# Two graph layers over sixteen graphs: in the first graph, turning through DRAM instead of by TensorE

## The chip, the core and the metric

One core of a Trainium2 chip runs the whole program. The metric is device time in microseconds (us) of one launch. Before the change it is 1216.43 us, the median of three runs (1216.17 to 1216.68).

## What is computed

Sixteen graphs of 1024 nodes with 256 features go through two layers, each with a residual and a layer norm. `adj` is symmetric and holds 0 and 1.

```
# layer 0, per graph
e0    = leaky_relu((h * a0) @ h.T, 0.2)               # 1024 x 1024, symmetric
alpha = sigmoid(where(adj == 1, e0, -max))            # kinds 2 to 4 do not occur
x     = layernorm(x + alpha @ h + bias)
# layer 1, per graph
Hh = x @ W;  s = Hh @ a_src;  d = Hh @ a_dst
e  = where(adj != 0, exp(-leaky_relu(s[:, None] + d[None, :], 0.2)), 0)
x  = layernorm(x + elu(e @ Hh / rowsum(e)))
```

## The kernel before, in words

All matrices are float32. A graph is cut into eight blocks of 128 nodes. `xs` holds the nodes as rows, `xTs` the features as rows (two chunks c of 128), `xas` is `xTs` times `a0`. Because the score matrix is symmetric, only its upper part is computed: `strip(b, jt)` makes block row jt from its diagonal to the right, in chunks of up to 512 columns. For each chunk TensorE makes `pe` (L254), ScalarE takes two tanh of it, `tb` (L262) and `low` (L263), and VectorE keeps the larger (L264). `finish` adds 1 and masks with `adj` into `al` (L270); GpSimd adds twice the identity on the diagonal block (`add_twice`, L284). The lower part of `al` is the strip turned over:

- In graphs 1 to 15 through DRAM. `dump` turns 32 by 32 blocks on VectorE (L290) and sends the strip off in four transfers whose runs are 32 elements long (L294); `gather` reads it back turned, in one transfer (L298); `mask` then adds 1 and masks in place (L305). `dump`, `gather` and most other transfers are issued by SyncE, whose queue is called SP here; they stand in it in the program's order, and an issue that waits holds up those behind it.
- In graph 0 by TensorE. `mirror` turns each 128 by 128 block with the identity into PSUM (L313), and VectorE masks from there (L315).

Graph 0 is done in the plain way. `multiply0(0, t)` sums row block t over eight blocks jt (L396), in the order jt = 0 to 7; for jt over t it reads what was turned. `end0` adds the bias (L405) and takes statistics. Strips run three ahead of the sums. The rows after layer 0's norm are `x1`. Layer 1 needs them turned: the upper half goes to DRAM (`save_x1`, L546), comes back in eight transfers with runs of 32 elements (`fetch_x1`, by `load_blocks`, L122), and VectorE turns the 32 by 32 blocks (`turn_x1`, L557). The lower half is turned by TensorE (`transpose_x1`, L564) and copied by ScalarE (L565). `scale0` normalizes `x1` in place on ScalarE, after `save_x1` has read it. Graph 1's `x` comes turned from DRAM by the same `load_blocks`, is finished on VectorE by `turn_x` (L213) and scaled on ScalarE (L219).

`W` gets two more columns (`make_Wx`: products with both halves of `a`, L188 and L189) and is then centred (`center_Wx`: two matrix products with a matrix of 1/256 into PSUM, L195, and two subtractions, L197).

From graph 1 on, layer 0 of graph b and layer 1 of graph b-1 run interleaved: strips with `project` (L582, layer 1's `x1 @ W`), then Strassen-like block products of `al` and `x` (L477) whose operands VectorE combines (L455), then layer 1's sums over `e` (L642), whose weights VectorE makes (L637). In graph 1, `project` starts at strip 2, behind `transpose_x1`.

The adjacency of a graph is 4 MB of int32, cast to bf16 by transfers that GpSimd issues (L107), on a queue of their own. Before the change those of graphs 0 and 1 are all issued at the start. The engines are scheduled by hand: instructions stand on each engine in the order of the program text.

Of the kernel before, what the change touches and what calls it, by code (L numbers as in the profile page):

```python
# [9 lines left out]
F32 = mybir.dt.float32  # L10
# [4 lines left out]
ALU = mybir.AluOpType  # L15
# [15 lines left out]
def one_kind_pass(  # L31
# [135 lines left out]
    for h in range(2):  # L167
        for g in range(2):
            load_adj(0, g, ts(h, HALF))
    for g in range(2):  # L170
        load_adj(1, g)

    acol = const.tile([P, ND], F32, tag="acol", name="acol")
    bcol = const.tile([P, ND], F32, tag="bcol", name="bcol")
# [13 lines left out]
            nc.vector.tensor_tensor(wprod, Wx[:, c, 2:], a_bc[:, ts(s, D)], ALU.mult)  # L188
            nc.vector.tensor_reduce(Wx[:, c, s : s + 1], wprod, AX.X, ALU.add)  # L189

    def center_Wx():

        pw = ps_t.tile([P, HT, P], F32, tag="t", name="pw").rearrange("p t q -> p (t q)")[:, 0 : D + 2]
        for c in range(ND):
            nc.tensor.matmul(pw, lhsT=mean_w, rhs=Wx[:, c, :], start=(c == 0), stop=(c == ND - 1))  # L195
        for c in range(ND):
            nc.vector.tensor_tensor(Wx[:, c, :], Wx[:, c, :], pw, ALU.subtract)  # L197

# [41 lines left out]
    def strip(b, jt):  # L240


        if jt == 0:
            als[b] = one.tile([P, NT, N], F32, tag="al", name=f"al_{b}")
        width = N - jt * P
        tb = four.tile([P, N], F32, tag="tb", name=f"tb_{b}_{jt}")
        tbs[b, jt] = tb
        n_chunks = -(-width // HALF)
        per = -(-(width // P) // n_chunks) * P
        for n, o in enumerate(range(0, width, per)):  # L250
            w = min(per, width - o)
            pe = ps_e.tile([P, HALF], F32, tag="e", name=f"pe_{b}_{jt}_{n}")
            for c in range(ND):
                nc.tensor.matmul(  # L254
                    pe[:, 0:w],
                    lhsT=xTs[b][:, c, ts(jt, P)],
                    rhs=xas[b][:, c, ds(jt * P + o, w)],
                    start=(c == 0),
                    stop=(c == ND - 1),
                )  # L260
            low = two.tile([P, HALF], F32, tag="low", name=f"low_{b}_{jt}_{n}")
            nc.scalar.activation(tb[:, ds(o, w)], pe[:, 0:w], AF.Tanh, scale=0.5)  # L262
            nc.scalar.activation(low[:, 0:w], pe[:, 0:w], AF.Tanh, scale=0.5 * SLOPE)  # L263
            nc.vector.tensor_tensor(tb[:, ds(o, w)], tb[:, ds(o, w)], low[:, 0:w], ALU.max)  # L264

    def finish(b, jt, c0=0, c1=N, ends=True):


        c0 = max(c0, jt * P)
        nc.vector.scalar_tensor_tensor(  # L270
            als[b][:, jt, c0:c1],
            tbs[b, jt][:, c0 - jt * P : c1 - jt * P],
            1.0,
            adjs[b, jt // HT][:, jt % HT, c0:c1],
            ALU.add,
            ALU.mult,
        )
        if ends and c0 == jt * P:
            add_twice(b, jt)
# [6 lines left out]
    def dump(b, t):  # L286


        tb = tbs[b, t][:, P : N - t * P]
        nc.vector.transpose(tb, tb)  # L290
        mirs[b, t] = dram.tile([N - (t + 1) * P, P], F32, tag=f"mir_{t}", name=f"mir_{b}_{t}")
        v = mirs[b, t].rearrange("(jb j) (a i) -> a j jb i", j=SQ, i=SQ)
        for a in range(P // SQ):
            nc.sync.dma_start(v[a], tb[ts(a, SQ), :].rearrange("p (jb i) -> p jb i", i=SQ))  # L294

    def gather(b, t):

# [131 lines left out]
    def scale0(b, t):  # L429
        scale(x1s[b][:, t, :], *r0s[b][t])  # L430
# [124 lines left out]
    def turn_x1(b, g):  # L555
        v = x1Ts[b][:, :, ts(g, HALF)]
        nc.vector.transpose(v, v)  # L557

    def transpose_x1(b):

        for c in range(ND):
            pt = ps_t.tile([P, HT, P], F32, tag="t", name=f"px1T_{b}_{c}")
            for t in range(HT):
                nc.tensor.transpose(pt[:, t, :], x1s[b][:, HT + t, ts(c, P)], ident)  # L564
            nc.scalar.copy(x1Ts[b][:, c, ts(1, HALF)], pt.rearrange("p t q -> p (t q)"))  # L565

    def project(b, t):

        if t == 0:
# [150 lines left out]

    for g in range(NT // 2):
        transpose_x(0, g)
    bias_bc = const.tile([P, D], F32, tag="bias", name="bias_bc")
# [6 lines left out]
    a_bc = y_kept[:, 0:2, :].rearrange("p t d -> p (t d)")  # L732
    nc.sync.dma_start(a_bc, a[0].partition_broadcast(P))
    Wx = const.tile([P, ND, D + 2], F32, tag="Wx", name="Wx")
    nc.sync.dma_start(Wx[:, :, 2:], W.rearrange("(c p) o -> p c o", p=P))
    strip(0, 0)
    strip(0, 1)
    for jt in range(2):
        finish(0, jt, 0, HALF)
        mirror(0, jt)  # L740
        if jt == 0:
            strip(0, 2)
    for t in range(NT):
        multiply0(0, t)
        for jt in ([0, 1], [2], [3])[t] if t < 3 else []:
            finish(0, jt, HALF, N)
        if t + 3 < NT:
            strip(0, t + 3)
        if t < 2:
            finish(0, t + 2, 0, HALF)  # L750
        elif t + 2 < NT:
            finish(0, t + 2)
        if t + 2 < NT - 1:
            mirror(0, t + 2)
        end0(0, t)
        if t < 2:
            make_Wx(t)
        if t == 4:
            center_Wx()
        if t == 1:  # L760
            new_xT(1)
            load_blocks(xTs[1], x[1], 0, N)
        if 1 <= t <= CHECKS:
            check_adj(0, t - 1)
        if t in (4, 5):
            turn_x(1, t - 4)
        if t == 3:
            save_x1(0, 0)
            fetch_x1(0, 0)
        if t in (5, 6):  # L770
            scale0(0, 2 * t - 10)
            scale0(0, 2 * t - 9)
    load_x(1, [nc.sync])

    for b in range(1, B):
        prev, done = b - 1, b - 2
        last = b == B - 1

        projects = [[], [0, 1], [2, 3], [4, 5], [6, 7], [], [], []]
        if prev == 0:  # L780

            projects = [[], [], [0, 1], [2, 3], [4, 5, 6, 7], [], [], []]
        for jt in range(NT):
            if jt == 4:
                mask(b, 0, 0, HT)
                combine_al(b, 1, 0, 2)
            if jt == 5:
                new_yT(b)
                product(b, 1)
                mask(b, 1, 0, HT)  # L790
                save_p(prev, 0, NT, nc.scalar)
                share_p(prev, 0, NT)
                combine_al(b, 1, 2, 3)
                mask(b, 0, HT)
                mask(b, 1, HT)
                mask(b, 2, 0, HT)
                combine_al(b, 1, 3, HT)
                mask(b, 2, HT)
                if done >= 0:
                    r1s[done] = center(mv1s[done], f"1_{done}", unit=1.0 / D)  # L800
            if jt == 6:
                unite(b, "p1")
                product(b, 5)
                unite(b, "p5")
                combine_al(b, 2, 0, HT)
            ahead = jt == 0 and b > 1
            if not ahead:
                strip(b, jt)
            if jt == 5:
                mask(b, 3, HT)  # L810
            if not ahead:
                finish(b, jt, ends=False)
            if jt == 4:
                gather(b, 3)
            if jt < NT - 1 and not ahead:
                dump(b, jt)
            if jt < 2 and done >= 0:
                deviation1(done, NT - 2 + jt)
            if prev == 0 and jt == 0:
                turn_x1(0, 0)  # L820
            if prev == 0 and jt == 1:
                transpose_x1(0)
            if ahead:
                gather(b, 0)
            if jt >= (1 if b == 1 else 2) and jt != 4:
                gather(b, jt - 1)
            if jt < 4 and b == 1:
                combine_x(b, jt)
# [653 lines left out]
```

## Time and profile before

| | |
|---|---|
| median of three runs | 1216.43 us |
| profiled execution, its own time | 1216.93 us |
| its span, first to last instruction | 1215.1 us |
| granted TensorE clock | 0.998 |
| TensorE busy | 1205.0 us |
| VectorE busy | 1003.9 us |
| ScalarE busy | 834.3 us |
| first instruction of graph 1's strips on TensorE | 53.7 us |
| last product of graph 1 (L477), first sum of layer 1 (L642) | 98.7 us, 102.1 us |

The span is cut into waits and work for each engine. An engine that is not on the chain of work that ended last may wait without cost, until what it is late with is needed. Two things change with the stage: in graph 0 TensorE is fed from x and the strips alone, with VectorE half busy; from about 60 us on VectorE is busy almost without a break while TensorE also is. Times are counted from the first instruction, so 1.8 us of the profiled execution lie outside the span.

### The profile page before, as it was taken

What the parts mean: (1) busy time and instruction counts of PE and PEld (TensorE: products, weight loads), DVE (VectorE), ACT (ScalarE), POOL (GpSimd) and SP (SyncE); (2) the same over time, 40 slices, a digit from 0 to 9 for tenths busy, and PEclk for the clock granted to TensorE, in tenths of its full rate; (3) what the DMA queues carried; (4) which work ended last, traced back from release to release, by engine and by line L of the source; (5) the groups of instructions that cost most, each with busy time, mean ns of one, the idle gap of its engine ahead of it and who ended that gap; (6) DMA issues with size and microseconds to landing.
All of it is one profiled execution on the core that took longest, in us unless ns stands there. A gap on an engine that the chain in (4) does not pass through costs nothing.

```text
span 1215.1 us, 15998 instructions
## 1 busy us (share of the span) xinstructions
PE 1205.0 (99%) x4385; PEld 819.4 (67%) x4385; DVE 1003.9 (83%) x1774; ACT 834.3 (69%) x2135; POOL 387.1 (32%) x715
## 2 busy tenths in 40 slices
PE   9999999999999999999999999999999999999997
PEld 7757657576575766757667586765757657576686
DVE  5698796988969789697897978979788896988957
ACT  4574866767677666775768757786676767767674
POOL 2320432504334142431414324143250433404343
PEclk9999999999999999999999999999999999999999
DMA  9568778697877878788787886878859788697412
GB/s 195 105 137 151 134 154 169 139 189 132 149 170 139 179 145 157 152 148 179 142 170 137 156 180 130 174 141 150 181 128 189 130 156 170 135 190 133 111 52 73
DMA packets 605080, 180.66 MB, mean 149 GB/s; under 512 B 482612, under 2 KB 587448, under 8 KB 604984
## 3 DMA queue, kind: packets, MB, share of 16 engines
q1 hardware_dynamic: 582800, 136.90, 56.4%
q0 software_dynamic: 20528, 41.95, 18.5%
q8 instruction: 37, 0.61, 0.2%
q10 hardware_dynamic: 1656, 0.72, 0.2%
q14 instruction: 59, 0.48, 0.1%
HBM read 152.44 MB, written 60.62 MB: 175 GB/s over the span
## 4 chain that ended last, share of the span: by engine, by line
PE 90%; DVE 3%; DMA 2%; ACT 2%; issue 1%; SPq 1%; POOL 0%; ACTq 0%; DVEq 0%; POOLq 0%
PE acc L642 33%; PE pe L254 18%; PE pH L582 8%; PE pV L477 8%; PE pQ L477 8%; PE pW L477 8%; PE pR L477 4%; PE acc L396 2%; DMA adj<-in_adjT 1%; DMA al<-mir 1%; DVE al L455 1%; DVE e L637 1%; ACT dev_junk L344 0%; DMA x<-y_rows 0%; DVE al L270 0%
## 5 line engine op out<-in xcount | busy, mean ns | idle before, releaser
L642 PE MATMUL acc<-H,e 128*128 128x257 f32 x2032 | 446.9, 380 | 0.0
L642 PEld LDWEIGHTS acc<-H,e 128*128 128x128 f32 x2032 | 385.1, 190 | 68.8 <-issue 13.9
L254 PE MATMUL pe<-xa,xT 128*128 128x384 f32 (+1 forms) x720 | 249.5, 486 | 0.1
L254 PEld LDWEIGHTS pe<-xa,xT 128*128 128x128 f32 x720 | 133.9, 190 | 91.8 <-issue 52.1
L264 DVE TENSOR_TENSOR tb<-tb,low 128x512 f32<-128x512 f32 (+1 forms) x192 | 112.6, 594 | 62.0 <-ACT low L263 60.1
L637 DVE SCALAR_TENSOR_TENSOR e<-p,pq_kept,adj 128x1024 f32<-128x1024 f32 (+1 forms) x136 | 159.9, 1229 | 0.1
L284 POOL TENSOR_TENSOR al<-ident,al 128x128 f32<-128x128 f32 x128 | 108.9, 864 | 143.1 <-DVE al L270 143.0
L455 DVE TENSOR_TENSOR al<-al 128x1024 f32<-128x1024 f32 (+2 forms) x105 | 143.7, 1369 | 5.1
L262 ACT ACTIVATE tb<-pe 128x512 f32<-128x512 f32 (+1 forms) x192 | 94.1, 490 | 76.6 <-PE pe L254 42.7
L130 ACT ACTIVATE junk<-adj,minus 128x2048 bf16<-128x2048 bf16 x64 | 127.4, 1991 | 0.0
L582 PE MATMUL pH<-Wx,yT 128*128 128x258 f32 x480 | 114.7, 381 | 0.6 <-ACT H L603 0.4
L104 POOL CAST adj<-x 128x1 bf16<-128x1 f32 x15 | 3.2, 213 | 351.6 <-DMA x<-y_rows 274.4
L582 PEld LDWEIGHTS pH<-Wx,yT 128*128 128x128 f32 x480 | 90.9, 190 | 26.7 <-issue 6.0
L477 PE MATMUL pV<-al,S 128*128 128x512 f32 x240 | 107.9, 592 | 0.0
L477 PE MATMUL pW<-al,x 128*128 128x512 f32 x240 | 107.9, 592 | 0.0
L477 PE MATMUL pQ<-al,x 128*128 128x512 f32 x240 | 107.9, 592 | 0.0
L270 DVE SCALAR_TENSOR_TENSOR al<-tb,adj 128x512 f32<-128x512 f32 (+7 forms) x132 | 97.4, 739 | 6.0 <-POOL mr L373 1.0
L668 ACT ACTIVATE sums<-acc,tiny 128x1 f32<-128x1 f32 x45 | 11.8, 262 | 128.0 <-PE acc L642 128.0
L687 ACT ACTIVATE h<-acc,rinv 128x256 f32<-128x256 f32 x81 | 38.2, 471 | 89.1 <-DVE rinv L679 78.1
L263 ACT ACTIVATE low<-pe 128x512 f32<-128x512 f32 (+1 forms) x192 | 95.0, 495 | 1.2 <-DVE tb L264 1.2
L305 DVE SCALAR_TENSOR_TENSOR al<-al,adj 128x512 f32<-128x512 f32 (+3 forms) x150 | 82.5, 566 | 11.7 <-DMA al<-mir 11.7
L477 PEld LDWEIGHTS pW<-al,x 128*128 128x128 f32 x240 | 45.6, 190 | 57.4 <-issue 55.2
(147 smaller groups left out, 1660.9 us busy)
## 6 DMA issues: line engine op xcount, KB each, us to landing
adj<-in_adjT POOLq DMA_DIRECT2D x30, 1024.0 KB, 8.3
x<-in_x SPq DMA_DIRECT2D x15, 1024.0 KB
y_rows<-Z SPq DMA_DIRECT2D x240, 64.0 KB
x<-y_rows SPq DMA_DIRECT2D x30, 512.0 KB
out<-y_kept SPq DMA_DIRECT2D x30, 512.0 KB
xT<-in_x SPq DMA_DIRECT2D x112, 128.0 KB
p<-p_row POOLq DMA_DIRECT2D x15, 512.0 KB, 4.1
mir<-tb SPq DMA_DIRECT2D x60, 112.0 KB
```

Source lines behind the costliest of these rows:

```text
L130: nc.scalar.activation(junk, rows, AF.Square, bias=minus1, scale=2.0, accum_out=chk[:, b * CHECKS + n : b * CHECKS + n + 1],)
L254: nc.tensor.matmul(pe[:, 0:w], lhsT=xTs[b][:, c, ts(jt, P)], rhs=xas[b][:, c, ds(jt * P + o, w)], start=(c == 0), stop=(c == ND - 1),)
L262: nc.scalar.activation(tb[:, ds(o, w)], pe[:, 0:w], AF.Tanh, scale=0.5)
L263: nc.scalar.activation(low[:, 0:w], pe[:, 0:w], AF.Tanh, scale=0.5 * SLOPE)
L264: nc.vector.tensor_tensor(tb[:, ds(o, w)], tb[:, ds(o, w)], low[:, 0:w], ALU.max)
L270: nc.vector.scalar_tensor_tensor(als[b][:, jt, c0:c1], tbs[b, jt][:, c0 - jt * P : c1 - jt * P], 1.0, adjs[b, jt // HT][:, jt % HT, c0:c1] ...
L284: nc.gpsimd.tensor_tensor(diag, ident2, diag, ALU.add)
L455: nc.vector.tensor_tensor(out_, in0, in1, ALU.subtract)
L477: nc.tensor.matmul(banks[bank], lhsT=lhs[:, jt, :], rhs=rhs[:, jt, :], start=first and jt == 0, stop=jt == HT - 1, skip_group_check=True,)
L582: nc.tensor.matmul(pt, lhsT=x1Ts[b][:, c, ts(t, P)], rhs=Wx[:, c, :], start=(c == 0), stop=(c == ND - 1),)
L637: nc.vector.scalar_tensor_tensor(e, p_bcs[b][:, cols], q, rows, ALU.mult, ALU.min)
L642: nc.tensor.matmul(acc, lhsT=es[b][:, m, ts(t, P)], rhs=Hs[b][m], start=(m == 0), stop=(m == NT - 1),)
```

## The change

1. Strips 1 to 6 of graph 0 are turned through DRAM. A new `dump_first` writes VectorE's turned blocks into a place of its own; `gather` and `mask` are those of the other graphs. Strip 0 keeps `mirror`. All strips and their turned copies of graph 0 live in one buffer, that of the later `e`.
2. Strips run five ahead of the sums, so strips 0 to 4 stand before the first sum.
3. Both halves of graph 0's `x1` go through DRAM. `transpose_x1` is gone; `turn_x1(0, 0)` comes at the end of graph 0's loop, `turn_x1(0, 1)` at graph 1's strip 2, and `project` starts one strip earlier.
4. `center_Wx` makes one product, of the sum of both chunks, which GpSimd adds (`add_Wx`). `make_Wx` comes at t = 3 and 4, the centring at t = 6.
5. Graph 1's adjacency is not issued at the start, but its two halves behind rows 1 and 5 of `x1`. Graph 1's turned x is loaded at t = 2 and finished at t = 5 and 6, one step later than before.

```diff
-    for g in range(2):
-        load_adj(1, g)
...
+    def add_Wx():
+        both = two.tile([P, HALF], F32, tag="low", name="both")[:, 0 : D + 2]
+        nc.gpsimd.tensor_tensor(both, Wx[:, 0, :], Wx[:, 1, :], ALU.add)
+        return both
+    def center_Wx(both):
...
-        for c in range(ND):
-            nc.tensor.matmul(pw, lhsT=mean_w, rhs=Wx[:, c, :], start=(c == 0), stop=(c == ND - 1))
+        nc.tensor.matmul(pw, lhsT=mean_w, rhs=both, start=True, stop=True)
...
+    def dump_first(t):
+        width = N - (t + 1) * P
+        tb = turned_home[:, ds(sum(N - (k + 1) * P for k in range(t)), width)]
+        nc.vector.transpose(tb, tbs[0, t][:, P : N - t * P])
+        mirs[0, t] = dram.tile([width, P], F32, tag=f"mir_{t}", name=f"mir_0_{t}")
+        v = mirs[0, t].rearrange("(jb j) (a i) -> a j jb i", j=SQ, i=SQ)
+        for a in range(P // SQ):
+            nc.sync.dma_start(v[a], tb[ts(a, SQ), :].rearrange("p (jb i) -> p jb i", i=SQ))
...
-    for jt in range(2):
-        finish(0, jt, 0, HALF)
-        mirror(0, jt)
-        if jt == 0:
-            strip(0, 2)
+    dump_first(1)
+    finish(0, 0, 0, HALF)
+    mirror(0, 0)
+    strip(0, 2)
+    dump_first(2)
+    gather(0, 1)
+    finish(0, 1, 0, HALF)
+    strip(0, 3)
+    dump_first(3)
+    gather(0, 2)
+    strip(0, 4)
+    dump_first(4)
+    gather(0, 3)
     for t in range(NT):
         multiply0(0, t)
+        if t + 1 < NT - 1:
+            mask(0, t + 1)
         for jt in ([0, 1], [2], [3])[t] if t < 3 else []:
             finish(0, jt, HALF, N)
-        if t + 3 < NT:
-            strip(0, t + 3)
+        if t + 5 < NT:
+            strip(0, t + 5)
+        if t + 5 < NT - 1:
+            dump_first(t + 5)
+        if t + 4 < NT - 1:
+            gather(0, t + 4)
...
-        if t + 2 < NT - 1:
-            mirror(0, t + 2)
         end0(0, t)
-        if t < 2:
-            make_Wx(t)
+        if t in (1, 5):
+            load_adj(1, t // 4, behind=x1s[0][:, t, 0:1])
+        if t in (3, 4):
+            make_Wx(t - 3)
         if t == 4:
-            center_Wx()
-        if t == 1:
+            both = add_Wx()
+        if t == 6:
+            center_Wx(both)
+        if t == 2:
             new_xT(1)
             load_blocks(xTs[1], x[1], 0, N)
...
-        if t in (4, 5):
-            turn_x(1, t - 4)
+        if t in (5, 6):
+            turn_x(1, t - 5)
         if t == 3:
             save_x1(0, 0)
             fetch_x1(0, 0)
...
+        if t == 7:
+            turn_x1(0, 0)
+    save_x1(0, 1)
     load_x(1, [nc.sync])
+    fetch_x1(0, 1)
...
-        if prev == 0:
-            projects = [[], [], [0, 1], [2, 3], [4, 5, 6, 7], [], [], []]
...
+            if prev == 0 and jt == 2:
+                turn_x1(0, 1)
...
-            if prev == 0 and jt == 0:
-                turn_x1(0, 0)
-            if prev == 0 and jt == 1:
-                transpose_x1(0)
```

More of the change, by code (lines that the diff above doesn't have):

```diff
@@ L189, in make_Wx @@
             nc.vector.tensor_reduce(Wx[:, c, s : s + 1], wprod, AX.X, ALU.add)
-    def center_Wx():
+    def add_Wx():
[3 more added lines that the diff above has]
+    def center_Wx(both):
         pw = ps_t.tile([P, HT, P], F32, tag="t", name="pw").rearrange("p t q -> p (t q)")[:, 0 : D + 2]
-        for c in range(ND):
-            nc.tensor.matmul(pw, lhsT=mean_w, rhs=Wx[:, c, :], start=(c == 0), stop=(c == ND - 1))
+        nc.tensor.matmul(pw, lhsT=mean_w, rhs=both, start=True, stop=True)
         for c in range(ND):
@@ L245, in strip @@
         width = N - jt * P
-        tb = four.tile([P, N], F32, tag="tb", name=f"tb_{b}_{jt}")
+        if b == 0:
+            tb = first_home[:, ds(sum(N - k * P for k in range(jt)), width)]
+        else:
+            tb = four.tile([P, N], F32, tag="tb", name=f"tb_{b}_{jt}")
         tbs[b, jt] = tb
@@ L294, in dump @@
             nc.sync.dma_start(v[a], tb[ts(a, SQ), :].rearrange("p (jb i) -> p jb i", i=SQ))
+    def dump_first(t):
[6 more added lines that the diff above has]
+            nc.sync.dma_start(v[a], tb[ts(a, SQ), :].rearrange("p (jb i) -> p jb i", i=SQ))
+    N_PE = 2
     def gather(b, t):
@@ L557, in turn_x1 @@
         nc.vector.transpose(v, v)
[L559 to L565, printed above, removed]
     def project(b, t):
@@ L718, in acc1 @@
         return pool.tile([P, D + 1], F32, tag=tag, name=f"acc1_{b}_{t}")
+    n_tb, n_turned = NT * (NT + 1) // 2 * P, NT * (NT - 1) // 2 * P
+    homes = one.tile([P, NT, N], F32, tag="ew", name="homes").rearrange("p t n -> p (t n)")
+    first_home, turned_home = homes[:, 0:n_tb], homes[:, n_tb : n_tb + n_turned]
     for g in range(NT // 2):
@@ L731, in one_kind_pass @@
     y_kept = const.tile([P, NT, D], F32, tag="y", name="y_kept")
-    a_bc = y_kept[:, 0:2, :].rearrange("p t d -> p (t d)")
+    a_bc = two.tile([P, NT, D], F32, tag="x1", name="a_home").rearrange("p t d -> p (t d)")[:, 0 : 2 * D]
     nc.sync.dma_start(a_bc, a[0].partition_broadcast(P))
```

## The prediction

> **What bounds the kernel now.** I read the page's shares first, then the chain of waits from 13 to 70 us, the timeline of that stretch, busy time by stage, and the transfer queues.
>
> ```profile
> PE 1205.0 (99%) x4385; PEld 819.4 (67%) x4385; DVE 1003.9 (83%) x1774; ACT 834.3 (69%) x2135; POOL 387.1 (32%) x715
> ```
>
> TensorE sets the time, so work taken from it counts in full unless it waits for something new. The chain (start, length, piece) has the pieces that go:
>
> ```profile
> 16.82 0.65 PE pal L313 x6
> ...
> 23.08 0.55 PE pal L313 x5
> ...
> 28.80 0.44 PE pal L313 x4
> ...
> 33.98 0.33 PE pal L313 x3
> ...
> 38.63 0.22 PE pal L313 x2
> ...
> 42.74 0.11 PE pal L313
> 42.85 0.87 PE pw L195 x4
> ...
> 60.53 0.87 PE px1T L564 x8
> ```
>
> The second engine is VectorE (columns PE, PEld, DVE, ACT, POOL):
>
> ```profile
> 81.70:112.00 30.30, 30.30 (x99) 18.23 (x98) 29.82 (x37) 12.45 (x20) 3.99 (x4) 1.00 0.71 115
> ```
>
> In graph 1 it idles 0.5 us of 30: what it gets late there, it hands on late. How far TensorE may run ahead of it I read at the product pV: VectorE's last subtraction for it (L455, 80.88 + 0.69) ends at 81.57, its fourth quarter uses it at 80.37 + 3 x 0.86 = 82.95. So the cover is about 1.3 us.
>
> The transfers of 14 to 17 us show how two queues share the 16 engines, those of 35 to 40 us how fast runs of 128 bytes go alone:
>
> ```profile
> q0 software_dynamic: 329, 0.33, 66.2%
> q1 hardware_dynamic: 327, 0.44, 47.9%
> ```
> ```profile
> DMA packets 6306, 0.80 MB, mean 159 GB/s; under 512 B 6306, under 2 KB 6306, under 8 KB 6306
> ```
>
> One packet for one, though unequal in length; alone 1250 packets per us. Beside a long adjacency packet a 128-byte one thus gets one turn in about 190 ns on each engine (adj packets of 2048 bytes take 173 ns), 85 per us over 16.
>
> **What goes.** 21 block transposes, 2.30 us (0.65 to 0.11 above); px1T, 0.87; half of pw, 0.44. Sum 3.61 us: without any new wait 1216.93 - 3.61 = 1213.3 profiled, 1212.8 as a median (the profiled execution lies 0.5 over it). ScalarE loses two copies (1.08), which TensorE's work hid.
>
> **What comes.** VectorE turns six strips: 0.98, 0.84, 0.71, 0.58, 0.45, 0.31 (L290, graph 1), 3.9 us, under graph 0's sums, where it is busy 32 of 50 us. Masking from SBUF costs as from PSUM (512 columns: 0.68 at L305 and at L315). One turn of x1 (1.2 us) leaves graph 1's full stretch for graph 0's end, another enters at strip 2. GpSimd's addition of the W chunks has no row; a 128x128 addition takes 0.46 and a 128x256 one-input operation 1.09, so 0.9 to 1.1; pw wants it only at t = 6. If that cover went, TensorE would wait by as much. The casts before the adjacency loads (0.2 to 0.45 each) have only diagonals and statistics behind them.
>
> *First new wait, strip 1's mirror.* Its last maximum ends at 14.97 (14.41 + 0.56); turned at 15.95. SP issues four transfers of 768 packets at once. Graph 1's dump of this size takes 4.2 us from first issue to last landing (66.77 to 70.97), its gather 3.5 (73.31 to 76.79). But ahead in the same queue is W, which lands at 18.63, and beside it graph 0's adjacency until 20.82. Sharing one for one, some 440 of 3072 packets go by 20.9; the rest takes 2630/1250 = 2.1, and 0.7 from last packet to landing (packet records of graph 1's dumps): 23.7. The gather is issued then and lands at 27.3; the first half of its mask (0.42) ends at 27.8. TensorE comes there at: strip 1 done 13.47, mirror 0 0.76, strips 2, 3, 4 2.58, 2.15, 1.72, sum 0 3.46, strip 5 1.29, two of eight parts of sum 1 0.86: 26.3. It waits 1.6 us. Bounds: 0 (the isolated 4.2 + 3.5 lands at 23.7) and 3.5 (the gather stands behind all of dump 2's 2560 packets, 2 us more). I take 1.6, as rows give each part. Later gathers have a sum of 3.5 us each for cover.
>
> [...]
>
> *What is late next.* VectorE stands at that mask from 23.3 to 27.3 (its rows up to there summed). Behind it wait, in order: mask 1.0, two halves of finish 1.3, strip 5's maximum 0.5 and turn 0.4, finish 0.4, end0 1.0, mask 0.9, finish 0.7, strip 6's maximum 0.4 and turn 0.3, finish 0.3, and row 1 of x1, 0.4. That row, 31.8 before, comes at 34.9 and releases the first half of graph 1's adjacency: packets from 36.9 (cast, issue and first packet 2.0) to 43.4 (8.2 us from issue to landing in a later graph). Meanwhile SP gets past gather 6 at 37.9 (strip 6 turned at 34.2, four issues of 0.45, landing at 37.4) and issues graph 1's turned x, 8192 packets: 300 go beside the adjacency, the rest needs 6.3 us alone, to 49.8. Row 5 of x1 is done at 46.8, GpSimd's cast after its W sum and a diagonal at 47.5, and the second half occupies the engines from 49.4 to 56. save_x1, issued at 43.8, lies in the queue behind x and so runs beside it.
>
> ```profile
> 40.94 0.39 SPq L546 DMA_DIRECT2D x_rows<-x  x1
> 43.89 5.09 SPq L122 DMA_DIRECT2D x1T<-x_rows  x8
> ```
>
> Alone (above: the fetch waits for the save) it takes 2.9 us, and the fetch 6.8 to its landing at 50.7. Here its 512 packets, 32 per engine, need 14 turns of 221 ns (173 + 48) after the adjacency's slow start: landing at 55.0. The fetch lands at 61.6.
>
> Two things stand behind that. ScalarE's scale0 waits for the save, and behind it is the second half of xas: 55.0 + 1.03 + 1.15 = 57.2, where strip 0 of graph 1 wants it at 51.35 + 1.6 + 0.86 = 53.8. And VectorE's turn of x1 (1.15) waits for the fetch, with every maximum of graph 1 behind it: done 62.8; two maxima, finish, turn, combination 4.25 (the same rows before): strip 1's first maximum at 67.0, before 63.45. That is 3.55 late, with the turn at strip 2 4.7. Less the cover of 1.3 and VectorE's 0.5 idle: TensorE leaves graph 1 2.9 us later than before. Its own lag at project (57.2 + 5.58 + 1.74 + 2.58 = 67.1 against 65.7) is smaller and does not add. save_x1's second half, load_x and its eight fetches now stand in SP ahead of dump(1, 0), which is ready at about 66.4 when SP is free at 66.7: they cost nothing then, but would hold it by several us if VectorE were on time.
>
> Sum: 1216.43 + 2.9 = 1219.3. The landing of the fetch is its soft term: 59.5 to 63.5 gives 1217.2 to 1221.4, the likeliest case's own range.
>
> **Rivals.**
>
> *All of it is gained.* If save and fetch run as alone and the mirror is in time, x lands by 46, the fetch by 55, VectorE is 2 us ahead in graph 1, and 3.6 us are saved: 1212.8. For it: strips run five ahead, 10.3 us from strip 1's turn to its use against 7.7 for an isolated dump and gather. Against it: the packet counts above, and that the second adjacency half is released just as x ends.
>
> *VectorE caps it.* The mirror comes in time, the save is only half slowed, fetch at 57.5: strip 1's first maximum at 62.9, 0.55 early, with the second turn 0.6 late, less the cover 1.3: 0.7 gained, 1215.7. For it: the 0.5 us idle of 30. Against: the wait at the mask.
>
> *Worse.* The gather stands behind dump 2 and the save is slowed at every packet (32 x 221 ns = 7.1, landing at 57.5): fetch at 64.3, VectorE 6.2 + 1.1 late, less 1.3: 6.0 lost, 1222.4.
>
> That the change doesn't do what it says I exclude: the order on TensorE has neither the transposes nor the second product.
>
> **How the numbers follow.** From no change a measurement here tells about 0.2%, 2.4 us: faster means under 1214.0, slower over 1218.9. Likeliest case 0.50 (0.38 of it slower, 0.12 same), everything gained 0.18, capped 0.22 (0.20 same, 0.02 faster), worse 0.10. That makes faster 0.20, same 0.32, slower 0.48. The range reaches down into the first rival and stops short of most of the worst: 1213.0 to 1221.8.
>
> **What would show it.** Right: TensorE idle 1 to 2.5 us inside graph 0's second sum, released by VectorE's mask; packets of save_x1 spread over some 5 us beside the adjacency; ScalarE waiting for the save before scale0; VectorE waiting 5 us or more for the fetch before turn_x1; few TensorE gaps after 112 us. Wrong: save_x1 landed within 3 us of x, fetch before 57, or TensorE unbroken through graph 1's first strips: then the first rival holds. If TensorE waits in graph 1 though the fetch was in time, for dump and gather, SP's order was the cost that I put at nothing.

## The result and the profile after

The changed kernel takes 1224.54 us, the median of six runs (1223.71 to 1226.77); the kernel before took 1216.34 beside it (six runs, 1215.78 to 1217.43). The ratio is 1.0069, 95% interval 1.0056 to 1.0082: slower by 8.2 us. The forecast was 1219.3, and its range ended at 1221.8. The profiled span grew by 7.8 us, from 1215.1 to 1222.9.

From here on, line numbers are those of the kernel that is shown. In the changed one L260 is a strip's product, L414 a sum of graph 0, L323 a mask, L222 the scaling of graph 1's x, L397 `scale0`, L564 `save_x1`, L122 `load_blocks` (turned x and fetch), L575 `turn_x1`, L592 `project`, and L473 and L495 the operands and products behind it.

The busy line of the page of the changed kernel:

```profile
PE 1202.9 (98%) x4354; PEld 816.2 (67%) x4354; DVE 1008.5 (82%) x1779; ACT 833.9 (68%) x2133; POOL 391.1 (32%) x718
```

TensorE has 31 instructions less and works 2.1 us less, so the work did go; the loss is idle time. TensorE's waits up to 130 us (waiting operation, what released it, us in total, times, longest):

```profile
PE pe L260 <- ACT xa L222: 7.1, 1, 7.1
PE acc L414 <- DVE al L323: 1.7, 1, 1.7
PE pV L495 <- DVE al L473: 1.2, 1, 1.2
PE pxT L233 <- DMA x<-in_x: 1.1, 1, 1.1
```

The kernel before had in the same stretch only 0.4 us at `pH` and 1.0 in front of its first instruction. Where the waits lie, in TensorE's timeline (start, length, operation, count, idle time before):

```profile
25.90 1.03 PE L414 MATMUL acc<-x,al 128*128 128x256 f32 x4
28.58 2.86 PE L414 MATMUL acc<-x,al 128*128 128x256 f32 x12 [1.66 <-DVE al L323]
...
53.74 1.02 PE L260 MATMUL pe<-xa,y_kept 128*128 128x512 f32 x2
61.90 7.53 PE L260 MATMUL pe<-xa,y_kept 128*128 128x512 f32 x14 [7.13 <-ACT xa L222]
```

The first wait is for the mirror of strip 1, in sum 1. The second, four times as long, stands inside strip 0 of graph 1: two instructions are done at 54.8, and the third wants the second half of the scaled x. What SP issued before that (start, time from the first issue to the end of the last):

```profile
37.99 11.05 SPq L122 DMA_DIRECT2D y_kept<-in_x  x8
49.13 0.80 SPq L564 DMA_DIRECT2D x_rows<-x  x1
59.70 4.12 SPq L122 DMA_DIRECT2D x1T<-x_rows  x8
```

Eight issues of graph 1's turned x hold SP for 11 us. Row 3 of x1, which the save waits for, was ready at 40.1, and the save was issued only at 49.13, right after them. The fetch waits for the save's landing, so its first issue marks that landing: 10.5 us after the save's issue, where the kernel before needed 2.9. What the queues moved from 51 to 54 us and from 54 to 57 us (packets, MB, share of 16 engines):

```profile
q0 software_dynamic: 218, 0.45, 96.5%
q1 hardware_dynamic: 35, 0.02, 2.9%
```
```profile
q0 software_dynamic: 222, 0.45, 80.8%
q1 hardware_dynamic: 219, 0.22, 27.2%
```

q0 carries the second half of graph 1's adjacency (issued at 48.69, landed at 59.03), q1 all that SP issues. At first SP's queue gets almost nothing (the save's 512 packets are 1 KB each, and at most 35 had gone by 54 us), then one packet for one, until the load runs out. Behind the save stands ScalarE, and behind the fetch VectorE (idle time before the instruction in brackets):

```profile
59.72 1.09 ACT L397 ACTIVATE x<-x,mr,r 128x256 f32<-128x256 f32 x2 [8.36 <-DMA x_rows<-x]
60.71 1.13 ACT L222 ACTIVATE xa<-y_kept,acol 128x1024 f32<-128x1024 f32 x1
```
```profile
65.96 1.25 DVE L575 STREAM_TRANSPOSE x1T<-x1T 128x1024 f32<-128x1024 f32 x1 [10.92 <-DMA x1T<-x_rows]
```

ScalarE's `scale0` waits 8.4 us for the save, and the scaling that TensorE wants stands behind it in the same queue. VectorE's turn of x1 comes at 65.96.

After the long wait TensorE is also slower: the 14 instructions took 7.53 us, where the same 14 take 5.85 in e1 and e5 below, behind waits of 1.1 and 0.2. Busy time of each engine and then the granted clock, by single microseconds:

```profile
57.00:58.00 1.00, 0.00 (x0) 0.00 (x0) 0.00 (x0) 0.00 (x0) 0.66 (x5) 1.00 1.07 271
58.00:59.00 1.00, 0.00 (x0) 0.00 (x0) 0.00 (x0) 0.00 (x0) 0.78 (x4) 0.75 0.34 111
59.00:60.00 1.00, 0.00 (x0) 0.00 (x0) 0.00 (x0) 0.28 (x1) 0.00 (x0) 0.50 0.02 6
...
64.00:65.00 1.00, 1.00 (x2) 0.44 (x2) 0.00 (x0) 0.99 (x2) 0.00 (x0) 0.50 0.78 127
65.00:66.00 1.00, 1.00 (x3) 0.36 (x2) 0.04 (x1) 0.09 (x1) 0.00 (x0) 0.84 1.07 334
66.00:67.00 1.00, 1.00 (x3) 0.40 (x3) 1.00 (x1) 0.54 (x2) 0.00 (x0) 1.00 1.04 278
```

The clock column reads 1.00, 0.75, 0.50 while TensorE idles, stays at 0.50 for 3.4 us after work is back at 61.90, and costs 1.7 us (7.53 for 5.85).

The account closes at graph 1's first product (L495; 75.48 us before, 82.69 after, +7.2). Strip 0 of graph 1 begins 0.2 earlier than before (53.74 for 53.92), with a start some 0.6 later (x landed late, as in some runs and not in others; graph 0's strips begin at 7.42 for 6.76 and end at 14.10 for 13.47) and the wait in sum 1 already in it; the wait adds 7.1, the clock 1.7, px1T and the 0.4 at `pH` are gone: -0.2 + 7.1 + 1.7 - 0.9 - 0.4 = 7.3. The wait at pV brings it to 8.7 at graph 1's second layer, and 0.9 of it is regained by the end.

### The profile page after: what moved, and what is told of

The parts are those of the page before. It is cut to its first block, busy times and chain, and to the rows that moved or that the text cites. A ratio compares the mean times of both kernels' runs of the same rounds, so it can differ in the third digit from the quotient of the medians.

```text
span 1222.9 us, 15992 instructions
## 1 busy us (share of the span) xinstructions
PE 1202.9 (98%) x4354; PEld 816.2 (67%) x4354; DVE 1008.5 (82%) x1779; ACT 833.9 (68%) x2133; POOL 391.1 (32%) x718
## 4 chain that ended last, share of the span: by engine, by line
PE 92%; DMA 3%; SPq 2%; DVE 2%; ACT 0%; issue 0%; ACTq 0%; DVEq 0%
PE acc L652 36%; PE pe L260 18%; PE pH L592 9%; PE pW L495 8%; PE pV L495 8%; PE pQ L495 8%; PE pR L495 4%; SPq L122 1%; DMA x<-in_x 1%; DMA x_rows<-x 1%; DMA al<-mir 1%; DMA mir<-homes 1%; SPq L310 0%; DVE al L276 0%; SPq L300 0%
## 5 line engine op out<-in xcount | busy, mean ns | idle before, releaser
L260 PE MATMUL pe<-xa,xT 128*128 128x384 f32 (+1 forms) x720 | 249.1, 486 | 0.0
L260 PEld LDWEIGHTS pe<-xa,xT 128*128 128x128 f32 x720 | 133.9, 190 | 91.7 <-issue 52.9
L473 DVE TENSOR_TENSOR al<-al 128x1024 f32<-128x1024 f32 (+2 forms) x105 | 143.8, 1370 | 5.2
L270 DVE TENSOR_TENSOR tb<-tb,low 128x384 f32<-128x384 f32 (+1 forms) x180 | 105.8, 596 | 44.9 <-ACT low L269 43.3
L268 ACT ACTIVATE tb<-pe 128x384 f32<-128x384 f32 (+1 forms) x180 | 88.2, 490 | 58.5 <-PE pe L260 32.3
L592 PE MATMUL pH<-Wx,yT 128*128 128x258 f32 x480 | 114.1, 380 | 0.0
L495 PE MATMUL pV<-al,S 128*128 128x512 f32 x240 | 108.4, 593 | 1.2 <-DVE al L473 1.2
L592 PEld LDWEIGHTS pH<-Wx,yT 128*128 128x128 f32 x480 | 91.1, 190 | 25.3 <-issue 6.5
L495 PE MATMUL pW<-al,x 128*128 128x512 f32 x240 | 107.9, 592 | 0.0
L495 PE MATMUL pQ<-al,x 128*128 128x512 f32 x240 | 107.9, 592 | 0.0
L323 DVE SCALAR_TENSOR_TENSOR al<-al,adj 128x512 f32<-128x512 f32 (+3 forms) x158 | 86.2, 561 | 21.7 <-DMA al<-mir 21.4
L276 DVE SCALAR_TENSOR_TENSOR al<-tb,adj 128x1024 f32<-128x1024 f32 (+3 forms) x120 | 90.9, 757 | 4.5
L495 PEld LDWEIGHTS pW<-al,x 128*128 128x128 f32 x240 | 45.6, 190 | 57.4 <-issue 54.9
```

The lines of the kernel that those rows point to most:

```text
L260: nc.tensor.matmul(pe[:, 0:w], lhsT=xTs[b][:, c, ts(jt, P)], rhs=xas[b][:, c, ds(jt * P + o, w)], start=(c == 0), stop=(c == ND - 1),)
L276: nc.vector.scalar_tensor_tensor(als[b][:, jt, c0:c1], tbs[b, jt][:, c0 - jt * P : c1 - jt * P], 1.0, adjs[b, jt // HT][:, jt % HT, c0:c1] ...
L473: nc.vector.tensor_tensor(out_, in0, in1, ALU.subtract)
L495: nc.tensor.matmul(banks[bank], lhsT=lhs[:, jt, :], rhs=rhs[:, jt, :], start=first and jt == 0, stop=jt == HT - 1, skip_group_check=True,)
L592: nc.tensor.matmul(pt, lhsT=x1Ts[b][:, c, ts(t, P)], rhs=Wx[:, c, :], start=(c == 0), stop=(c == ND - 1),)
```

## The experiments

Theory T: the second adjacency half starves the save of x1, and all follows from that. Rival R1: the mirrors' round trips through DRAM are the cost, in sum 1 and in VectorE's longer queue. Rival R2: x1's second half, which also went to DRAM, is the cost. The changed kernel and the twelve experiments in one table; waits are TensorE's in the profiled execution, in us; the last column is the start of graph 1's first product. Each ratio is to the kernel before as it ran beside that experiment (medians from 1216.3 to 1217.5), so two experiments are compared by their ratios, where a step of 0.001 is 1.2 us.

| kernel | median | ratio to before, 95% | sums | strip 0/1 | projections | pV | product |
|---|---|---|---|---|---|---|---|
| changed kernel | 1224.54 | 1.0069, 1.0056 to 1.0082 | 1.7 | 7.1 | 0 | 1.2 | 82.69 |
| e1 late half | 1224.03 | 1.0059, 1.0045 to 1.0073 | 1.7 | 1.1 | 5.1 | 1.0 | 81.43 |
| e2 adjacency at start | 1226.68 | 1.0079, 1.0065 to 1.0093 | 10.4 | 0 | 0 | 1.0 | 83.66 |
| e5 scale0 later | 1227.10 | 1.0079, 1.0065 to 1.0092 | 1.8 | 0.2 | 8.7 | 2.0 | 84.40 |
| e7 x1 half by TensorE | 1224.93 | 1.0065, 1.0051 to 1.0079 | 1.8 | 8.2 | 0.4 | 0 | 84.83 |
| e8 = e1 and e7 | 1220.45 | 1.0027, 1.0016 to 1.0038 | 1.7 | 1.1 | 2.0 | 0 | 79.47 |
| e3 before, adjacency moved | 1217.86 | 1.0006, 0.9997 to 1.0016 | 0 | 0.2 | 0.8 | 0 | 76.39 |
| e6 mirrors by TensorE | 1216.72 | 0.9994, 0.9984 to 1.0004 | 0 | 0 | 0 | 1.2 | 73.76 |
| v1 late mirrors only | 1215.02 | 0.9984, 0.9974 to 0.9994 | 0 | 0.6 | 0 | 0.4 | 73.68 |
| e13 x by GpSimd | 1220.21 | 1.0030, 1.0018 to 1.0042 | 3.6 | 0 | 0.2 | 1.2 | 75.85 |
| e15 save by GpSimd | 1223.01 | 1.0051, 1.0037 to 1.0064 | 0.3 | 6.7 | 0 | 0 | 82.63 |
| e18 e6 with x late | 1229.70 | 1.0101, 1.0085 to 1.0116 | 0 | 8.8 | 0 | 0.2 | 86.69 |
| e20 x by ScalarE | 1221.96 | 1.0036, 1.0022 to 1.0050 | 4.8 | 0 | 0.8 | 1.5 | 79.79 |

### e1: the second adjacency half released later

```diff
-        if t in (1, 5):
-            load_adj(1, t // 4, behind=x1s[0][:, t, 0:1])
+        if t == 1:
+            load_adj(1, 0, behind=x1s[0][:, t, 0:1])
...
         if t == 7:
             turn_x1(0, 0)
+            load_adj(1, 1, behind=x1Ts[0][:, 0, 0:1])
```

> Only the second half of graph 1's adjacency is moved: it waits for x1's turned first half (65.96 us in the changed kernel) instead of for row 5 of x1 (48.7 us). Theory T (this load starves the save of x1, and the late save holds ScalarE's scaling of graph 1's x, for which TensorE idles 7.1 us and then runs strip 1 at a lower clock): save landed within 6 us of its issue instead of 10.5, fetch landed before 60.5 instead of 65.84, TensorE's wait at strip 1 of graph 1 under 3 us instead of 7.1, no slice at a clock of 0.5, 1217 to 1220.5 us. Rival R1 (the round trips of the mirrors are the main cost): 1223.5 or more, unchanged within 1 us. Rival R2 (x1's second half on SP's queue is the cost): 1223.5 or more as well.

TensorE's waits:

```profile
PE pH L592 <- DVE x1T L575: 5.1, 1, 5.1
PE acc L414 <- DVE al L323: 1.7, 1, 1.7
PE pe L260 <- ACT xa L222: 1.1, 1, 1.1
```

All that T said of the first half came true: the save landed 4.2 us after its issue, the fetch at 59.5, and the wait at the strip fell to 1.1. The time did not follow. The load, issued at 61.78 now, met the fetch of x1's second half: its transfers issued at 61.52 and 61.90 landed at 65.97 and 66.37, those issued from 62.43 on only at 71.8 to 73.2, and the projections wait 5.1 us for that half. The wait moved from one half to the other, and the clock fell to 0.50 behind it (74.2 to 77.6). The time alone, 1224.03, is what R1 and R2 had forecast; it is the landings that speak for T. The starving is confirmed, but here it took the fetch, which now lay beside the load.

### e2: the adjacency at the start again

```diff
-        if t in (1, 5):
-            load_adj(1, t // 4, behind=x1s[0][:, t, 0:1])
...
+    for g in range(2):
+        load_adj(1, g)
```

> Both halves of graph 1's adjacency are loaded at the start again, as before the change; the rest of the change stays. Theory T: the save and fetch of x1 run undisturbed (save under 4.5 us, fetch landed before 58), TensorE waits under 1 us at graph 1's strip 1, but the dump and gather of mirror 1 share the queues with the adjacency until about 31 us, so sum 1 waits 5 to 8 us instead of 1.7: 1217 to 1222 us. R1: slower than the changed kernel, 1226 or more. R2: 1224 or more.

As T said, x1 ran undisturbed and the strips did not wait. But sum 1 waited more than T allowed, and the time, 1226.68, is where R1 and R2 had it and not T:

```profile
PE acc L416 <- DVE al L325: 10.4, 1, 10.4
```

The dump of mirror 1, issued from 16.46 on, landed only at 29.1 to 33.0, around the adjacency's last landing at 31.3. So the mirrors' round trip does cost TensorE when a load lies beside it; the move of the adjacency is what mirror 1 needs, and it cannot simply be undone.

### e5: scale0 behind graph 1's strips

```diff
-        if t in (5, 6):
-            scale0(0, 2 * t - 10)
-            scale0(0, 2 * t - 9)
...
             if prev == 0 and n < 2:
+                scale0(0, 2 * n)
+                scale0(0, 2 * n + 1)
```

> The scaling of x1's rows 0 to 3 on ScalarE (which waits until the save has landed) is moved behind graph 1's strips, so that graph 1's second x half is scaled at once. No DMA moves. If T is right in that TensorE's own wait decides (7.1 us, and some 1.8 us of lowered clock behind it): the wait at strip 1 falls under 1.5 us and the time to 1217 to 1219.5 us, less what VectorE's late turn of x1 (65.96 us) then costs. If the prediction's chain decides after all (save, fetch, VectorE's turn of x1, its maximum of strip 1): VectorE still waits for the fetch near 65 us and the time falls by no more than 1.5 us, to 1223 or more. R1: unchanged within 1 us.

No gain, which the side of T had not expected: 1227.10, 2.6 us above the changed kernel by the medians, 1.2 by the ratios, whose intervals overlap, so that no loss is shown either. The profiled execution is the slowest of the five (1229.03). The wait at the strip is 0.2; TensorE then stands 8.7 us at the projections instead, 7.1 of it at the first, since the fetch still landed at 66.1:

```profile
54.60 5.85 PE L260 MATMUL pe<-xa,y_kept 128*128 128x512 f32 x14 [0.17 <-ACT xa L222]
67.51 3.49 PE L592 MATMUL pH<-Wx,x1T 128*128 128x258 f32 x8 [7.06 <-DMA x_rows<-x]
70.84 2.74 PE L260 MATMUL pe<-xa,y_kept 128*128 128x384 f32 x8
```

VectorE's turn of it ends at 67.46, just before the first projection; the releaser that the line names is not it. TensorE's clock falls again: the 8 products at 67.51 take 3.49 us, the next 8, at 73.42, take 1.91. Strip 2 begins at 70.84, where the changed kernel begins it at 71.01. So the prediction's chain (save, fetch, VectorE's turn) bounds TensorE as tightly as ScalarE's does: the two end within 0.2 us of each other. Further on pV waits 2.0 instead of 1.2, and behind it the clock falls a second time (0.50 from 94.4 to 97.9); the stretch from graph 1's first product to its second `pQ` is 23.7 us long instead of 21.3. Whether the four scalings, moved into that stage, made the longer wait was not tested.

### e7 and e8: x1's second half by TensorE again, alone and with e1

```diff
-    save_x1(0, 1)
     load_x(1, [nc.sync])
-    fetch_x1(0, 1)
...
+            if prev == 0 and jt == 1:
+                transpose_x1(0)
```

> The second half of x1 is turned by TensorE again (8 transposes, two evictions on ScalarE, no second save and fetch, graph 1's projections as before the change). R2 (the second half through DRAM is the cost): 1221 or less. T: the starved first save is untouched, TensorE does 0.87 us more and the wait for the second half goes: 1223.5 to 1225.5 us. R1: the same, 1223.5 to 1225.5 us.

> The last edit of the adjacency (second half released by x1's turned first half) together with x1's second half turned by TensorE again, so that no transfer that the strips need lies beside that load. Theory T2 (whatever SP has in flight when a GpSimd-issued adjacency half begins waits some 7 us; alone, each of the two edits only hands the wait to the other half of x1): waits of TensorE at strip 1 of graph 1 and at the projections under 1.5 us together, and so 1217 to 1219.5 us. If the wait moves once more (rival R3: TensorE's lead is bounded by VectorE's backlog in graph 1, not by these transfers): VectorE's late mirrors make TensorE wait at graph 1's first products instead, 1221.5 or more.

Alone it changes nothing (1224.93): R2 is out. Together with the late half it is 4 us under the changed kernel, 1 short of what T2 gave; the projections wait 2.0 us for ScalarE and sum 1 still 1.7. Behind that short wait the clock falls too (0.50 from 77.0 to 80.4): the projection takes 3.27 us for 1.91 and the product after it 4.07 for 3.60, 1.8 us in all, which is more than what T2 missed by. One more reading comes from these two: the pV wait is nought in both, in e3 and before the change, in all kernels in which TensorE turns the second half, while it is 1.0 to 2.0 in most of those that fetch it.

### e3: the kernel before with only the adjacency moved

```diff
-    for g in range(2):
-        load_adj(1, g)
...
+        if t in (1, 5):
+            load_adj(1, t // 4, behind=x1s[0][:, t, 0:1])
```

> The kernel before with one thing changed: graph 1's adjacency is released by rows 1 and 5 of x1. All transposes stay on TensorE. T2: the first half lies beside graph 1's turned x and the second beside x1's save, so that TensorE waits 4 to 8 us at graph 1's strip 1 here as well: 1220 to 1224.5 us. R1 (the mirrors' round trips are the cost): within 1 us of the kernel before, 1217.5 or less.

T2 fell here: 1.0006, no loss that can be told from nothing. The turned x was issued from 33.97 on and was slowed by the first half, but the save was issued at 45.23 and landed at 49.88, 1.3 us after the second half was issued, and so escaped it. The fetch was caught (landed at 60.5), but projections start one strip later in this kernel, and TensorE's waits there grew only from 0.4 to 0.8. The loads alone are harmless; something must bring x1's save to them.

### e6: the changed kernel with graph 0's mirrors by TensorE

```diff
-    dump_first(1)
-    dump_first(2)
-    gather(0, 1)
...
+    for jt in range(2):
+        finish(0, jt, 0, HALF)
+        mirror(0, jt)
```

> The changed kernel with graph 0's seven mirrors on TensorE again, its strips three ahead as before; the adjacency at rows 1 and 5, x1's halves through DRAM and the one product stay. T2: the wait in sum 1 (1.7 us) goes, 2.3 us of transposes come back, SP has 24 dumps and 6 gathers less ahead of the turned x, but the second adjacency half still meets the save: 1221 to 1225 us. R1: 1219 or less.

This is outside what T2 allowed: the mirrors, not the adjacency alone, carry the loss, in so far R1 is right. (The run also puts graph 0's strips back to three ahead of the sums; e13 below keeps them five ahead.) How they do is in SP's issues:

```profile
18.58 6.40 SPq L122 DMA_DIRECT2D y_kept<-in_x  x5
41.09 0.39 SPq L564 DMA_DIRECT2D x_rows<-x  x1
44.03 5.48 SPq L122 DMA_DIRECT2D x1T<-x_rows  x8
```

With no dumps and gathers in SP's queue, the turned x is issued by 25 us (the line has the last five of its eight issues) and the save at 41.09; it lands in 2.9 us, long before the second half. That made theory T3: the dumps and gathers push the turned x back to 38 us, behind the first adjacency half; its slow issues push the save to 49; there it meets the second half.

### e18 and e13: T3 from both sides

e18 is e6 with the turned x held back by hand, without any mirror in DRAM:

```diff
+        if t == 3:
+            new_xT(1)
+            nc.gpsimd.tensor_copy(xTs[1][:, 0, 0:1], x1s[0][:, 3, 0:1])
+            load_blocks(xTs[1], x[1], 0, N)
```

> The run with the mirrors on TensorE (1216.7 us) with one thing added: graph 1's turned x is held until row 3 of x1 (about 41 us instead of 23.6). No mirror goes through DRAM. T3: the turned x fills SP's queue until about 49, the save is issued there and lands at 57 to 60 beside the second adjacency half, TensorE waits 5 to 8 us at strip 1 of graph 1: 1221.5 to 1225.5 us, the whole loss of the change without its mirrors. R1: within 1.5 us of 1216.7.

e13 is the changed kernel, all mirrors in DRAM, with the turned x out of SP's queue:

```diff
+        if t == 1:
+            new_xT(1)
+            load_blocks(xTs[1], x[1], 0, N, nc.gpsimd)
         if t in (1, 5):
             load_adj(1, t // 4, behind=x1s[0][:, t, 0:1])
```

> The changed kernel with one thing moved: the eight transfers of graph 1's turned x are issued by GpSimd after row 0 of x1, in the same queue as and ahead of the first adjacency half, instead of by SP behind the mirrors' dumps and gathers. All mirrors stay in DRAM. Theory T3 (what costs is the chain on SP: dumps and gathers push the turned x behind the first adjacency half, that pushes the save of x1 onto the second): turned x landed by 41 us instead of 52.2, save issued by 46 and landed by 50 instead of 59.6, wait at strip 1 of graph 1 under 1.5 us instead of 7.1, up to 3 us at the projections from the fetch beside the second half, 1216 to 1220 us. If the mirrors cost by themselves (R1: wait in sum 1, VectorE's longer queue): 1222.5 or more.

SP's issues in e18, and then in e13:

```profile
46.53 11.94 SPq L122 DMA_DIRECT2D y_kept<-in_x  x8
58.57 0.55 SPq L564 DMA_DIRECT2D x_rows<-x  x1
62.60 4.03 SPq L122 DMA_DIRECT2D x1T<-x_rows  x8
```
```profile
39.45 0.36 SPq L564 DMA_DIRECT2D x_rows<-x  x1
45.30 7.62 SPq L122 DMA_DIRECT2D x1T<-x_rows  x8
```

In e18 a late turned x alone makes the wait at the strip, 8.8 us, and 13 us of loss against e6, more than the 1221.5 to 1225.5 expected. It came later than intended (46.5 for 41), as the copy that holds it stood behind other work of GpSimd, and so e18 doesn't rebuild T3's last link: the second half, issued at 48.54, caught the turned x itself, whose last piece landed at 61.5, and 6.6 of the 8.8 us are TensorE's wait for the first half of x. The other 2.3 are its second half, turned by 62.75 and then behind `scale0` in ScalarE's queue. The save was issued at 58.57, after that load had landed (57.07), and took 4.0 us. What e18 shows is that a late turned x costs this much without any mirror in DRAM; that the save meets the load is shown by the changed kernel and e1. In e13 the save is issued at 39.45 and landed at 45.2, and the wait at the strip is gone, with all 21 blocks still turned through DRAM; the ratio falls from 1.0069 to 1.0030. T3's local numbers held but one, the last piece of x, which landed at 46.5 instead of 41; the time, 1220.21, missed T3's bound by 0.2 and lies under R1's 1222.5. What is left in e13 are these waits:

```profile
PE acc L414 <- POOL al L290: 2.3, 1, 2.3
PE acc L414 <- DVE al L323: 1.3, 1, 1.3
PE pV L495 <- DVE al L473: 1.2, 1, 1.2
```

The first is a diagonal that GpSimd added late, being busy with the eight issues. Its six runs fall into two groups (1218.6 to 1219.2 and 1221.3 to 1222.0); the profile is of the first, and why there are two stays open.

### e15 and e20: other queues

```diff
         if t == 3:
-            save_x1(0, 0)
+            save_x1(0, 0, nc.gpsimd)
```

> The changed kernel with the first save of x1 issued by GpSimd, ahead of the second adjacency half in the same queue, instead of by SP behind the turned x. Bytes and all else are the same. T3: the save lands by 50 us instead of 59.6, so ScalarE scales graph 1's second x half in time and the wait at strip 1 falls under 1.5 us from 7.1; the fetch stays on SP beside the second half and lands at 58 to 61 instead of 65.8, for which the projections wait 2 to 5 us: 1217.5 to 1221.5 us. If the load's bandwidth is the limit and not the place in the queue: save and fetch as late as before, 1223 or more.

```diff
+        if t == 0:
+            new_xT(1)
+            load_blocks(xTs[1], x[1], 0, N, nc.scalar)
```

> The changed kernel with one thing moved: graph 1's turned x is issued by ScalarE in the first step of the sums (about 27 us), on a queue that holds neither the dumps nor GpSimd's additions; in the run where GpSimd issued it, TensorE waited 2.3 us for a diagonal that GpSimd added late. All mirrors stay in DRAM. T3: turned x landed by 38 us, before the first adjacency half; save issued by 46 and landed by 50; wait at strip 1 of graph 1 under 1 us; the wait for GpSimd gone and 1.3 to 2.5 us left in sum 1; 1216 to 1219 us, about the kernel before: what the mirrors save is given back in sum 1 and in graph 1's products. If the remaining 3.6 us of the GpSimd run belong to the mirrors as such (R1): 1220 or more.

Both missed their times, as the wait moved again. In e15 the save, ahead of the adjacency in GpSimd's queue, landed at 50.6, near the 50 expected; the last two pieces of the turned x, issued at 48.55 and 50.30, were caught instead and landed at 58.7 and 59.5, and the strip waits for them 6.7 us. In e20 x landed by 39.7 and the strip does not wait, but x now lies beside the gather of mirror 2:

```profile
PE acc L414 <- DVE al L323: 4.8, 2, 3.7
PE pV L495 <- DVE al L473: 1.5, 1, 1.5
```

Mirror 2's gather was issued at 31.46 (27.72 in the changed kernel), just as a piece of x landed, and landed itself at 36.3; sum 2 waits 3.7 us, and the clock falls behind it (37.5 to 40.9). ScalarE, which had eight issues to make, did no strip work for 8.4 us. The time, 1221.96, is in the range that had been given to R1, so e20 doesn't clear the mirrors of the rest. In every run with all of them in DRAM somebody waits, whatever the order; that there is more to move between 16 and 50 us than these queues move in time is my reading, not shown by itself.

### v1: what the readings suggest

Graph 1's adjacency at the start as before the change, mirrors 1 and 2 by TensorE as well as mirror 0, mirrors 3 to 6 and x1 through DRAM, one centring product, x one row earlier.

```diff
-    dump_first(1)
...
+    mirror(0, 1)
...
-        if t + 1 < NT - 1:
+        if 3 <= t + 1 < NT - 1:
             mask(0, t + 1)
...
+        if t == 0:
+            mirror(0, 2)
```

> Built from the readings so far: graph 1's adjacency at the start as before the change, mirrors 1 and 2 (which would meet it) by TensorE, mirrors 3 to 6 and both halves of x1 through DRAM, graph 1's turned x one row earlier. T2: dump 3 lands by 33 us, sum 3 waits under 1 us, the save is issued and landed by 49, no wait at strip 1; 10 mirror transposes, 8 of x1 and half a product less, 2.4 us: 1213.5 to 1216 us. If DRAM turns cost more than they save wherever they lie (R1): 1218 or more.

```profile
PE pe L262 <- ACT xa L224: 0.6, 1, 0.6
PE pV L497 <- DVE al L475: 0.4, 1, 0.4
```

1215.02 against 1217.48 beside it, ratio 0.9984, and the interval leaves out 1: the one version that beats both kernels. It drops 10 of 21 mirror blocks (1.1 us by the chain of the kernel before), px1T and half of pw, 2.4 in all, and gives back 1.0 in waits; 0.4 at `pH` is gone too. That makes 1.8, where the ratio gives 1.9 and the profiled spans 2.4 (1215.1 and 1212.7).

## Why the prediction failed

- *What goes, 3.61 us*: right. TensorE's busy time fell by 2.1 though the clock added 1.7, 3.8 together.
- *First new wait, 1.6 us*: right, 1.66. Dump 1 landed at 24.8 and its gather at 28.1, 1.1 and 0.8 later than worked out, with a start 0.6 later, so TensorE came later as well. Row 1 of x1 came at 35.2 (34.9), the first half landed at 45.0 (packets to 43.4).
- *"SP issues graph 1's turned x ... to 49.8", "save_x1, issued at 43.8"*: the first step that failed. I let SP issue eight transfers in a row and wait only for the engines. Two of the eight issues took 2.9 and 3.3 us while the first adjacency half was under way, all eight 11.05, and x landed at 52.2. The save went out at 49.13, 5.3 us late.
- *"14 turns of 221 ns (173 + 48) after the adjacency's slow start: landing at 55.0"*: the second. The sum let 18 of the 32 packets per engine pass before the load was at speed. In the run it was the other way round: of the 512 at most 35 had gone by 54 us, then 219 went one for one in 3 us (the price of a turn was right), and the save landed at 59.63, 0.6 us after the load. Of the 4.6 us by which that is late, 2.4 are x (52.2 for 49.8) and 2.2 the save behind it (7.4 us for 5.2). The fetch landed at 65.8 instead of 61.6 (the prediction's own 55.0 + 6.8 makes 61.8), outside the 59.5 to 63.5 given for it.
- *"Its own lag at project is smaller and does not add"*: the third, and the one that chose the wrong engine. TensorE's own wait for the scaled x (57.2 promised, 61.8 measured) was 7.1 us and set its lag; VectorE, with strip 1's first maximum at 72.1 instead of 67.0, then cost only the 1.2 at pV. The mechanism named in the prediction (scale0 behind the save, x behind scale0) was right and its size was not (a wait of 3.4 us, from 53.8 to 57.2, that was to cost less than VectorE's lag); e5 shows that VectorE's chain ends only 0.2 us away, so the wrong choice of the engine alone cost the forecast little.
- *What no term had*: the halved clock after the wait, 1.7 us (7.53 us for 5.85).
- *"They cost nothing then"* (the second half of x1 ahead of dump(1, 0)): VectorE had turned that strip at 70.8, SP was free at 72.7 and issued at 73.2, 2.3 us later. e6, where SP holds that dump only 0.5 us, also pays 1.2 at pV, more than the 0.87 that px1T gives; how much of the 1.2 is SP's order and how much VectorE's second turn of x1, no run separates.
- *Rivals*: "worse" came nearest (fetch 64.3, 1222.4), and by the same two transfers; its 7.1 us for the save is close to the 7.4 from x's landing to the save's; "all is gained" and "VectorE caps it" fell with the save's landing. The sign was right for the reason given, the size was not.

With the measured sizes the sum is: 3.6 removed, 1.7 + 7.1 + 1.7 + 1.2 added, 8.1 us net, where the medians differ by 8.2 and the profiled spans by 7.8 (the later start adds 0.6, 0.9 is regained behind graph 1). Against e6 the mirrors in DRAM cost 9 us by the ratios. Of this the runs show some 4.7 to be the place of the turned x in SP's queue (e13 against the changed kernel, by the ratios; 4.3 by the medians). The rest, some 4.4, was not split further; R1 is not out for it.

## What to carry over

Before a turn is moved from TensorE to DMA, write down the whole queue of the issuer with issue times, not only the moved transfers: here 24 dumps and 6 gathers made TensorE wait 1.7 us themselves, and made a load behind them late, which made a save late, which stalled ScalarE and then TensorE. Keep a transfer on which an engine's queue hangs from being in flight when a large load starts on another queue; if it can't be kept, reckon with the load's whole length (8.7 to 10.3 us in the table below), even if the transfer is short (64 KB there). And undoing one part proves little while the wait can move to the next transfer (e1, e5, e15): take the suspect away entirely (e6), put its effect back by other means (e18), and look in the trace whether the effect is the same one: in e18 it was only in part.

## What the runs showed of the hardware

*The adjacency loads on GpSimd's queue held most of what SP had in flight.* Each row is a transfer that SP issued around the start of an adjacency half (1 MB); alone, the save took 2.9 us, a piece of the fetch 2.2 to 3.2 and one of the turned x 2.6 to 4.3 behind its like (kernel before).

| run | adjacency issued, landed | SP's transfer | issued | landed |
|---|---|---|---|---|
| changed kernel | 48.69, 59.03 | save, 512 KB | 49.13 | 59.63 |
| e1 | 61.78, 71.46 | fetch, 64 KB | 61.90 | 66.37 |
| e1 | 61.78, 71.46 | fetch, 64 KB | 62.43 | 71.79 |
| e6 | 48.43, 57.59 | fetch, 64 KB | 48.50 | 50.72 |
| e6 | 48.43, 57.59 | fetch, 64 KB | 49.03 | 57.80 |
| e3 | 48.59, 57.26 | fetch, 64 KB | 49.90 | 57.60 |
| e15 | 49.30, 58.01 | turned x, 128 KB | 46.99 | 52.04 |
| e15 | 49.30, 58.01 | turned x, 128 KB | 48.55 | 58.66 |

In these rows, what SP's queue had not landed within 2.3 to 4.6 us of the load's issue landed 0.2 to 0.7 us behind the load, 64 KB or 512. Small pieces got through a little earlier: in the changed kernel the gather of mirror 5 (128 KB) landed at 43.59, 1.4 us before the first half, in e20 a dump of 16 KB 2.7 us before it. In the changed kernel the trace has 222 and 219 packets of the two queues from 54 to 57 us (one for one, at the prediction's 221 ns, would make 217); the three us before, with 218 and 35, don't fit that. Why a load keeps the other queue out at its start, no run shows.

*SP's issues were stretched beside a load*, from 0.3 to 1.0 us to 2.9 and 3.3 (changed kernel), 4.7 (e3, e18).

*TensorE's clock fell after idling, in e8 behind a wait of only 2.0 us.* Spells at half clock lasted 6.8 us in the changed kernel (58.5 to 65.3, wait 7.1), 10.2 in e2 (wait 10.4), 3.4 in e1 (74.2 to 77.6, wait 5.1), but also 3.4 in e20 (37.5 to 40.9, wait 3.7) and in e8 (77.0 to 80.4, wait 2.0); e13's wait of 2.3 brought none. The spell began 3.7 us after the last product in the changed kernel, 4.5 in e1, 4.6 in e20 and 2.6 in e8; in the last two TensorE was at work again by then. What sets a spell's start and its length, no run shows. The spell cost 1.4 us (e7, 7.25 for 5.85) to 1.8 (e8) on top of the wait.
